# Bidirectional Mamba block: first pairs reordered, polynomial bank changed

## The chip, the cores and the metric

The kernel runs on one core of a Trainium2 chip. The metric is the device time of one execution in microseconds. A core has five engines that run their own instruction queues: TensorE (PE; its weight loads are shown as PEld), VectorE (DVE), ScalarE (ACT), GpSimd (POOL) and SyncE (SP), which here issues most transfers. They wait for each other by semaphores only. TensorE writes to PSUM, 8 banks of 2 KB per partition; GpSimd does not read PSUM in this kernel.

## What is computed

A batch of 8 sequences, 512 tokens, 256 channels, in float32. For each sequence:

```python
x = x + attn(layernorm(x))          # two Mamba2 directions, joined by Wo, bo
x = x + ffn(layernorm(x))           # x @ W.T + b + (x @ V_r) @ C.T

# one direction (the other runs over the flipped sequence)
zxbcdt = x @ Win                                   # 256 -> 512 z, 640 xBC, 8 dt
xBC = silu(conv4_causal_depthwise(xBC) + convb)    # xs 512, B 64, C 64
dt  = softplus(dt + dtb);  dA = exp(dt * -exp(Alog))     # 8 heads
h_t = dA_t * h_(t-1) + dt_t * B_t (x) x_t          # state 64 x 64 per head
y_t = C_t . h_t + D * x_t
y = y * silu(z);  y = y * rsqrt(mean(y*y) + 1e-5) * normw
return y @ Wout
```

## The kernel before, in words

A sequence is cut into 4 chunks of 128 tokens. A **pair** (class `Pair`, L461) is chunk c of the forward direction with chunk 3 - c of the backward one; there are 32 pairs, 4 per sequence. Within a chunk the recurrence is done as matrix products: `lam` (L478) is the decay dA broadcast over 128 partitions for 8 heads, `scan` (L505) turns it into a 128x128 decay matrix per head on VectorE, `cb` (L533) forms the products of C and B on TensorE, `mix` (L544) multiplies both on VectorE, and `outputs` (L582) applies them to `xdt` (x times dt, `scale_x`, L522, GpSimd). Between chunks a state `h` is carried: `add_state`, `new_state`, `decay_state` (L574 to L618), and `dec` (L484, scaled by C in `scale_c`, L498) carries it into the outputs. `evict` (L620, VectorE) adds the skip term, which `skip` (L549, ScalarE) has put into `yg`; `times_gate` (L624, GpSimd) multiplies by the gate, which `gate` (L557, TensorE) and `gate_silu` (L569, ScalarE) have made.

A **Block** (L388) is 128 channels of the xBC projection of one direction over the whole sequence: block 4 holds B and C, blocks 0 to 3 hold x. `project` is TensorE (L401), `tap` (L411, ScalarE) does the first conv tap out of PSUM, `convolve` (L414) the other three on VectorE, or `convolve_aside` (L424) does them as three ScalarE products and three GpSimd additions. `silu` (L434) follows on ScalarE, for a whole block of 512 tokens. While the pairs of one sequence run, the ten blocks of the next are made, spread by the table `share` (L826 to L833).

Step sizes are made for two sequences at a time (class `Steps`, L308): softplus by a polynomial of 9 terms on VectorE (`ratio`, L318, and `series`, L326), whose intermediates z and u lie in one PSUM bank, `pzu` (L319); then `exponential` on ScalarE and `decays` (L340), which writes the decays to DRAM; from there the broadcasts `lam` and `dec` are fetched by SP (`fetch`, `fetch_dec`).

A **Tail** (L650) is one finished chunk of 128 tokens: the output product with `wy` (L664), which is Wout, normw and Wo multiplied beforehand in `prepare_wy` (L196), then residual, second norm and the feed-forward product.

PSUM: one bank holds the identity `seed` for the scans; `p_proj` has 3 banks, `p_tr` (transposes, cb, small things) 2, `p_y` 2. A pool gives out the bank whose release was recorded first, so the order of the program decides which release a matmul waits for.

Nothing is planned at run time. The order on each engine is the order in which the program is written, fixed by `pin` (L60): first the start (L721 to L820), which norms sequence 0 (L724 to L733), transposes it (L738), makes its blocks and the step sizes of sequences 0 and 1, and prepares pair 0; then the loop over the pairs (L849), which finishes pair i and prepares pair i + 1. SP's queue is in order too: the loads of weights (`load_weights`, L178) put two of them, `wot`, into buffers of the pool of `lam`, so later `lam` fetches wait until those are free.

Of the kernel before, what the change touches and what calls it, by code (L numbers as in the profile page):

```python
# [14 lines left out]
P = 128  # L15
# [16 lines left out]
def tile_bimamba_ffn(  # L32
# [163 lines left out]
    def prepare_wy(d, blks):  # L196

        wot, wo_sb = staged[d]
        for blk in blks:
            pw = ps(p_y, [P, DM], f"pwy_{d}_{blk}")  # L200
            for k in range(NK):
                pe.matmul(
                    pw, lhsT=wot[:, k, blk * P:(blk + 1) * P], rhs=wo_sb[:, k, :],
                    start=(k == 0), stop=(k == NK - 1),
                )
            dve.tensor_scalar(wy[:, d, blk, :], pw, normw_sb[:, d, blk:blk + 1], None, ALU.mult)
# [18 lines left out]

    def scales(mv, n, name):

        rs = small.tile([P, n], F32, name=f"{name}_rs", tag=f"lnrs{n}")
        nm = small.tile([P, n], F32, name=f"{name}_nm", tag=f"lnnm{n}")
        pool.tensor_scalar(rs, mv[:, :, 1], 1.0, EPS, ALU.mult, ALU.add)  # L230
        pool.tensor_tensor(rs, rs, neghalf[:, :n], ALU.pow)
        pool.tensor_tensor(nm, mv[:, :, 0], rs, ALU.mult)
        pool.tensor_scalar(nm, nm, -1.0, None, ALU.mult)
        return rs, nm
# [73 lines left out]
    class Steps:  # L308
# [9 lines left out]
        def ratio(m):  # L318
            pzu = ps(p_tr, [P, 2, P], f"pzu_{m.b0}")  # L319
            m.z, m.u = pzu[:, 0, :], pzu[:, 1, :]  # L320
            dve.tensor_scalar(m.z, m.e, 2.0, None, ALU.add)
            dve.reciprocal(m.r, m.z)
            dve.tensor_tensor(m.e, m.e, m.r, ALU.mult)
            dve.tensor_tensor(m.u, m.e, m.e, ALU.mult)
# [136 lines left out]
    class Pair:  # L461
# [51 lines left out]

        def turn(m, d):
# [18 lines left out]
        def cb(m):  # L533

            m.pcb = [ps(p_tr, [P, P], f"cb_{m.name}_{d}") for d in range(2)]
            for u in range(2):
                for d in range(2):
# [19 lines left out]
        def gate(m, d):  # L557
            if d == 0:
                m.sz = m.tile("sz", (P, 2, NBLK, P))
# [7 lines left out]
            m.pz = pz  # L567

        def gate_silu(m, d):  # L569
            act.activation(m.sz[:, d], m.pz, AF.Silu)  # L570
# [79 lines left out]
    class Tail:  # L650
# [37 lines left out]
        def norm2_v(t):  # L688

            rs = small.tile([P, 1], F32, name=f"ln2_{t.name}_rs", tag="lnrs1")  # L690
            pool.tensor_scalar(rs, t.mv[:, :, 1], 1.0, EPS, ALU.mult, ALU.add)
            pool.tensor_tensor(rs, rs, neghalf[:, :1], ALU.pow)
# [33 lines left out]
    for c0 in range(0, NC, 2):  # L726
        mv = statistics(xh[:, c0:c0 + 2], 2, f"ln1_0_{c0}")
        halves.append(scales(mv, 2, f"ln1_0_{c0}"))
    for half, (rs, nm) in enumerate(halves):
        c = 2 * half  # L730
        act.activation(xh[:, c, :], xh[:, c, :], AF.Identity, bias=nm[:, 0:1], scale=rs[:, 0:1])
        c += 1
        dve.tensor_scalar(xh[:, c, :], xh[:, c, :], rs[:, 1:2], nm[:, 1:2], ALU.mult, ALU.add)  # L733
# [9 lines left out]
    for j in range(NC):  # L743
        dve.tensor_copy(seed[:, j * P:(j + 1) * P], ident)

    def projected(*key):
        first[key].project(p_y if key[1] in (2, 3) else None)
        first[key].tap()


    act.activation(a_col, a_col, AF.Exp)
    dve.tensor_scalar(a_col, a_col, -1.0, None, ALU.mult)
    projected(0, NBLK)
    stats1(1, 0)
    stats1(1, 2)
    scales1(1)
    projected(0, 0)
    norm1(1)
    projected(0, 1)
    first[0, NBLK].convolve()  # L760
    projected(0, 2)
    pdt = ps(p_y, [P, P], "pdt_0")
    steps_direct(pdt, 0, 0)
    for k in range(NK):
        turn1(1, k)
    first[0, 1].convolve_aside()
    first[0, 0].convolve()
# [3 lines left out]
    first[0, 2].convolve()  # L771
    st.ratio()
    first[0, 3].convolve_aside()
    st.series()
    projected(1, NBLK)
    projected(1, 0)
    st.exponential()
    first[1, NBLK].convolve()
# [10 lines left out]
    first[0, NBLK].silu()  # L789
    first[1, 1].convolve_aside()  # L790
    projected(1, 2)
    first[1, 0].convolve()
    projected(1, 3)
    for blk in range(NBLK):
        first[0, blk].silu()
    q.gate(0)
    steps_by_token(0)
    q.turn(0)
    first[1, NBLK].silu()
    first[1, 2].convolve()  # L800
    q.cb()
    q.scale_x(0)
    q.gate_silu(0)
    first[1, 0].silu()
    first[1, 3].convolve()
    q.gate(1)
    q.scan(0)
    first[1, 1].silu()
    first[1, 2].silu()
    first[1, 3].silu()  # L810
    q.turn(1)
    q.scale_x(1)
    q.gate_silu(1)
    q.skip(0)
    q.mix(0)
    q.scan(1)
    tokenwise_b(0)
# [7 lines left out]
    for b in range(1, NB):  # L825
# [5 lines left out]
        for bb, c, m in share:  # L831
            todo[bb, c] = [Block(b, *blocks[k + j]) for j in range(m)]
            k += m  # L833
    ends = [(b, c) for b in range(NB) for c in (1, 2, 0, 3)]
# [14 lines left out]
    for i in range(n):  # L849
# [19 lines left out]
        p.decay_state()  # L869
        if q:  # L870
            q.scale_c()
# [15 lines left out]
        when(work[0], "project", "tap")  # L887
# [25 lines left out]
        if i < 2:  # L913
            prepare_wy(i, range(2))
# [10 lines left out]
        when(before, "norm_power")  # L925
        p.presum()
# [15 lines left out]
        if i < 2:  # L942
            prepare_wy(i, range(2, NBLK))
        elif i == 2:
            prepare_wf()
        when(work[1], "convolve")
        if i == 0:
            steps_last(0)
            steps_total(0)
# [7 lines left out]
        if q:  # L957
            q.gate(1)
            q.gate_silu(1)
        if even and c in (1, 3) and ahead < NB:  # L960
            turn1(ahead + (c == 3), 0)
            turn1(ahead + (c == 3), 1)
        if q:
            q.skip(1)
        if c == 2 and b + 1 < NB:
            tokenwise_b(b + 1)
        for w in work[2:]:
            when(w, "project", "tap")
        when(work[1], "silu")
        for w in work[2:]:  # L970
            when(w, "convolve")
        if b == 0:
            when(work[3], "silu")
# [3 lines left out]
        late, before = work[2], p  # L977
# [66 lines left out]
```

## Time and profile before

| | |
|---|---|
| time, median of 3 runs | 638.48 us (638.48 to 639.05) |
| the profiled execution | 640.16 us, of which its span 638.4 us |
| TensorE clock granted, mean | 0.99 |
| busy: PE, DVE, POOL, ACT | 96%, 85%, 73%, 61% of the span |
| chain that ended last | PE 72%, DVE 13%, POOL 6%, ACT 4% |
| 0 to 48 us: PE, DVE, ACT, POOL busy | 34.16, 33.48, 29.55, 21.12 us |
| 48 to 110 us: the same | 61.12, 58.65, 40.89, 39.77 us |

The span runs from the first to the last instruction; the time has 1.8 us more around it. The profile names an instruction by line, engine, operation and its tiles, out<-in. A wait is put down to what ended last before the instruction could start. The busy share of an engine is an average over stages, so what counts is which engine the others wait for in each stage; the slices and the busy time by stage show that.

### The profile page before, as it was taken

The page shows a single profiled execution, that of the slowest core. Times are in us where ns is not written, and L with a number is a line of the kernel's source. Part 1 is how long each engine was busy: PE and PEld are TensorE (multiplying, and loading weights), DVE is VectorE, ACT ScalarE, POOL GpSimd, SP SyncE. Part 2 cuts the span into 40 slices and gives each one's busy share as a digit, 9 for nine tenths or more (in the row PEclk, how much of TensorE's full clock was granted, in tenths as well). Part 3 has the DMA queues.
Part 4 walks back from the last instruction along what each step waited for, and adds up shares of the span by engine and source line. Part 5 has one row for each costly group of instructions (what it writes and reads, how often), then busy time and mean ns, then how long its engine had stood idle before and what let it go on. Part 6 is the DMA issues. An engine that isn't in the chain of part 4 may idle for free.

```text
span 638.4 us, 12802 instructions
## 1 busy us (share of the span) xinstructions
PE 612.1 (96%) x4772; PEld 459.5 (72%) x4772; DVE 542.4 (85%) x827; ACT 392.3 (61%) x845; POOL 464.6 (73%) x570
## 2 busy tenths in 40 slices
PE   4979999999999999999999999999999999999896
PEld 2547677678777787767777787767777778788784
DVE  4798999989999988888999989887999998866733
ACT  2787656767676465766776574774786665644431
POOL 3548664778767895867857897766868788589982
PEclk9989999999999999999999999999999999999998
DMA  7464432035055423017056322107026232343011
GB/s 217 143 195 139 132 101 49 2 103 166 1 190 150 116 83 116 17 32 223 18 160 164 102 94 77 59 20 216 18 55 204 66 99 83 117 138 96 16 51 34
DMA packets 36254, 64.87 MB, mean 102 GB/s; under 512 B 8608, under 2 KB 23392, under 8 KB 36192
## 3 DMA queue, kind: packets, MB, share of 16 engines
q1 hardware_dynamic: 34048, 64.00, 33.3%
q8 instruction: 38, 0.62, 0.4%
q10 hardware_dynamic: 2144, 0.04, 0.2%
q14 instruction: 24, 0.20, 0.1%
HBM read 59.12 MB, written 4.72 MB: 100 GB/s over the span
## 4 chain that ended last, share of the span: by engine, by line
PE 72%; DVE 13%; POOL 6%; ACT 4%; issue 3%; DMA 1%; ACTq 0%; POOLq 0%; DVEq 0%
PE pp L401 18%; PE pm L669 14%; PE pz L563 14%; PE py L588 8%; PE pf L709 4%; PE pxs L518 4%; DVE lam L512 3%; DVE xc L419 2%; PE pst L608 2%; PE ss L634 2%; PE cb L539 2%; DVE lam L545 1%; DVE r L330 1%; POOL yg L626 1%; POOL xdt L529 1%
## 5 line engine op out<-in xcount | busy, mean ns | idle before, releaser
L419 DVE SCALAR_TENSOR_TENSOR xc<-pp,conv_sb,xc 128x511 f32<-128x511 f32 x183 | 135.8, 745 | 28.0 <-ACT xc L412 23.6
L401 PE MATMUL pp<-xhT,win_sb 128*128 128x512 f32 x320 | 151.3, 600 | 0.5 <-ACT xhT L739 0.5
L512 DVE TENSOR_TENSOR_SCAN lam<-lam,seed 128x512 f32<-128x512 f32 x128 | 145.6, 1200 | 0.0
L563 PEld LDWEIGHTS pz<-xhT,win_sb 128*128 128x128 f32 x1024 | 123.3, 194 | 10.6 <-issue 9.4
L563 PE MATMUL pz<-xhT,win_sb 128*128 128x128 f32 x1024 | 126.9, 278 | 0.0
L669 PE MATMUL pm<-wy,yg 128*128 128x256 f32 x512 | 115.6, 379 | 0.0
L669 PEld LDWEIGHTS pm<-wy,yg 128*128 128x128 f32 x512 | 97.1, 190 | 13.3 <-issue 0.2
L401 PEld LDWEIGHTS pp<-xhT,win_sb 128*128 128x128 f32 x320 | 57.6, 193 | 45.9 <-issue 43.3
L553 ACT ACTIVATE yg<-xc,dcol 128x128 f32<-128x128 f32 x256 | 81.3, 395 | 0.0
L412 ACT ACTIVATE xc<-pp,conv_sb 128x512 f32<-128x512 f32 x64 | 49.5, 777 | 47.4 <-PE pp L401 47.4
L545 DVE TENSOR_TENSOR lam<-lam,cb 128x1024 f32<-128x1024 f32 x64 | 75.0, 1212 | 0.3
L529 POOL TENSOR_TENSOR xdt<-xs,dw 128x512 f32<-128x512 f32 x64 | 66.5, 1045 | 6.5 <-ACT xs L520 6.4
L588 PE MATMUL py<-lam,xdt 128*64 128x128 f32 x1024 | 63.0, 276 | 0.0
L588 PEld LDWEIGHTS py<-lam,xdt 128*64 128x64 f32 x1024 | 55.2, 137 | 9.2 <-issue 3.1
L622 DVE TENSOR_TENSOR yg<-py,yg 128x512 f32<-128x512 f32 x64 | 42.0, 684 | 14.9 <-PE py L588 13.2
L529 POOL TENSOR_TENSOR xs<-xs,dw 128x512 f32<-128x512 f32 x48 | 50.1, 1043 | 3.8
L676 DVE SCALAR_TENSOR_TENSOR x<-pm,rms,x 128x256 f32<-128x256 f32 x64 | 30.8, 482 | 18.5 <-PE pm L669 8.2
L638 ACT ACTIVATE rms<-ss,eps_col 128x2 f32<-128x2 f32 x32 | 8.4, 262 | 61.9 <-PE ss L634 61.8
L437 ACT ACTIVATE xc<-xc 128x512 f32<-128x512 f32 x64 | 39.4, 626 | 11.0 <-DVE xc L419 10.9
L518 PE MATMUL pxs<-ident,xc 128*128 128x128 f32 x256 | 39.1, 285 | 6.8 <-ACT xc L437 4.2
L230 POOL TENSOR_SCALAR ln_rs<-ln_mv 128x1 f32<-128x1 f32 (+2 forms) x39 | 7.5, 192 | 48.9 <-DVE ln_mv L223 47.9
L520 ACT COPY xs<-pxs 128x512 f32<-128x512 f32 x64 | 35.9, 589 | 11.4 <-PE pxs L518 11.4
(446 smaller groups left out, 999.3 us busy)
## 6 DMA issues: line engine op xcount, KB each, us to landing
lam<-dat SPq DMA_DIRECT2D x64, 512.0 KB
x<-in_x_dram SPq DMA_DIRECT2D x36, 128.0 KB
out_dram<-x SPq DMA_DIRECT2D x32, 128.0 KB
x<-in_x_dram SPq DMA_DIRECT2D x7, 512.0 KB
win_sb<-in_win_dram SPq DMA_DIRECT2D x2, 640.0 KB
win_sb<-in_win_dram SPq DMA_DIRECT2D x2, 512.0 KB
wot<-in_wout_t_dram SPq DMA_DIRECT2D x2, 512.0 KB
rows<-raw SPq DMA_DIRECT2D x48, 4.0 KB
```

Source lines behind the costliest of these rows:

```text
L401: pe.matmul(pp, lhsT=win_sb[:, d, k, c0:c0 + P], rhs=s["xhT"][:, k, :], start=(k == 0), stop=(k == NK - 1),)
L412: act.activation(self.acc, self.pp, AF.Identity, bias=self.w[:, 4:5], scale=self.w[:, 3:4])
L419: dve.scalar_tensor_tensor(self.acc[:, to], self.pp[:, of], self.w[:, 3 - j:4 - j], self.acc[:, to], ALU.mult, ALU.add,)
L512: dve.tensor_tensor_scan(lam, lam, sd, 0.0, ALU.mult, ALU.add)
L518: pe.transpose(pt[:, blk * P:(blk + 1) * P], m.s["xc", d][:, blk, m.tcol[d]], ident)
L529: pool.tensor_tensor(hb(to), hb(m.xw[d]), dw[:, j, cols].unsqueeze(2).to_broadcast([P, NH, HD]), ALU.mult)
L545: dve.tensor_tensor(m.lam[d], m.lam[d], m.pcb[d].unsqueeze(1).to_broadcast([P, NH, P]), ALU.mult)
L553: act.activation(yg[:, blk, :], m.s["xc", d][:, blk, m.tcol[d]], AF.Copy, scale=dcol[:, d, blk:blk + 1])
L563: pe.matmul(pz[:, blk, :], lhsT=win_sb[:, d, k, blk * P:(blk + 1) * P], rhs=m.s["xhT"][:, k, m.tcol[d]], start=(k == 0), stop=(k == NK - 1),)
L588: pe.matmul(m.py[d][two * HD:(two + 1) * HD, blk, :], lhsT=lhsT, rhs=rhs, start=first, stop=last, skip_group_check=True,)
L622: dve.tensor_tensor(yg, m.py[d], yg, ALU.add)
L669: pe.matmul(t.pm[:, d, :], lhsT=yg[:, blk, :], rhs=wy[:, d, blk, :], start=(blk == 0), stop=(blk == NBLK - 1),)
```

## The change

- **First norm.** Sequence 0 is normed wholly on VectorE, as (x - mean) times the inverse deviation, instead of two chunks on ScalarE and two on VectorE as x times scale plus offset. The offsets are not made any more. The four copies of the identity into `seed` go from VectorE to ScalarE.
- **Start reordered.** The statistics of sequence 1 stand ahead of the multiplication of `a_col`; `tap` and `convolve` are called apart from `project`; block 1 of the forward direction is convolved on VectorE, block 3 of the backward one aside; the convs of the backward direction come after `decays`.
- **Silu of x by chunk.** For sequence 0 the silu of x is done chunk by chunk (`silu_x`, all four blocks of 128 tokens at once), for pairs 0 and 1 in the start, for pairs 2 and 3 at the end of the loops two pairs earlier.
- **Output weights ahead.** `prepare_wy` makes two blocks in one bank. Direction 0 is made in the start, its scaling on ScalarE; direction 1 in the first loop; `prepare_wf` moves from the third loop to the second. The first block of sequence 1 is projected and tapped in the start (`ahead`).
- **Within sequence 0's loops.** `scale_c` comes after the scans, `decay_state` at the end of the loop before, one block of sequence 1 is convolved aside in the first loop, and its B and C blocks get their silu one loop later ("late").
- **Polynomial.** For the sequences after the first two, `pzu` is taken from `p_proj` instead of `p_tr`.
- `cb` issues direction 0's two products before direction 1's; `m.pz` keeps both gates' banks.

```diff
-    def prepare_wy(d, blks):
+    def prepare_wy(d, blks, aside=False):
         wot, wo_sb = staged[d]
-        for blk in blks:
-            pw = ps(p_y, [P, DM], f"pwy_{d}_{blk}")
+        pw = ps(p_y, [P, 2, DM], f"pwy_{d}_{blks[0]}")
+        for j, blk in enumerate(blks):
...
+            if aside:
+                act.activation(to, pw[:, j, :], AF.Copy, scale=scale)
+            else:
+                dve.tensor_scalar(to, pw[:, j, :], scale, None, ALU.mult)
...
         def ratio(m):
-            pzu = ps(p_tr, [P, 2, P], f"pzu_{m.b0}")
+            pzu = ps(p_proj if m.b0 else p_tr, [P, 2, P], f"pzu_{m.b0}")
...
+        def silu_x(m, d):
+            x = m.s["xc", d][:, :, m.tcol[d]]
+            act.activation(x, x, AF.Silu)
...
-    for half, (rs, nm) in enumerate(halves):
-        c = 2 * half
-        act.activation(xh[:, c, :], xh[:, c, :], AF.Identity, bias=nm[:, 0:1], scale=rs[:, 0:1])
-        c += 1
-        dve.tensor_scalar(xh[:, c, :], xh[:, c, :], rs[:, 1:2], nm[:, 1:2], ALU.mult, ALU.add)
+    for half, (mv, rs) in enumerate(halves):
+        for j in range(2):
+            c = 2 * half + j
+            dve.tensor_scalar(xh[:, c, :], xh[:, c, :], mv[:, j, 0:1], rs[:, j:j + 1], ALU.subtract, ALU.mult)
...
-    for j in range(NC):
-        dve.tensor_copy(seed[:, j * P:(j + 1) * P], ident)
+    for j in range(NC):
+        act.copy(seed[:, j * P:(j + 1) * P], ident)
     act.activation(a_col, a_col, AF.Exp)
-    dve.tensor_scalar(a_col, a_col, -1.0, None, ALU.mult)
-    projected(0, NBLK)
     stats1(1, 0)
     stats1(1, 2)
     scales1(1)
+    projected(0, NBLK)
+    tap(0, NBLK)
...
     projected(0, 3)
-    first[0, 2].convolve()
+    tap(0, 3)
     st.ratio()
     first[0, 3].convolve_aside()
+    projected(1, NBLK)
+    tap(1, NBLK)
     st.series()
-    projected(1, NBLK)
     projected(1, 0)
+    tap(1, 0)
     st.exponential()
-    first[1, NBLK].convolve()
     st.decays()
     st.weigh()
...
-    for blk in range(NBLK):
-        first[0, blk].silu()
+    q.silu_x(0)
+    first[0, NBLK].silu()
+    first[1, 3].convolve_aside()
     q.gate(0)
+    q.gate(1)
     steps_by_token(0)
     q.turn(0)
+    conv(1, 2)
+    q.scale_x(0)
     first[1, NBLK].silu()
-    first[1, 2].convolve()
+    prepare_wy(0, (0, 1), True)
+    tokenwise_b(0)
     q.cb()
-    q.scale_x(0)
     q.gate_silu(0)
-    first[1, 0].silu()
-    first[1, 3].convolve()
-    q.gate(1)
+    q.silu_x(1)
     q.scan(0)
-    first[1, 1].silu()
-    first[1, 2].silu()
-    first[1, 3].silu()
+    pairs[1].silu_x(0)
+    prepare_wy(0, (2, 3), True)
     q.turn(1)
+    ahead = Block(1, *blocks[0])
+    ahead.project()
     q.scale_x(1)
     q.gate_silu(1)
+    pairs[1].silu_x(1)
+    ahead.tap()
+    steps_last(0)
     q.skip(0)
...
+        if i + 2 < NC:
+            for d in range(2):
+                pairs[i + 2].silu_x(d)
...
-        when(work[1], "silu")
-        for w in work[2:]:
-            when(w, "convolve")
-        if b == 0:
-            when(work[3], "silu")
+        if i:
+            when(work[1], "silu")
+        if q and q.b == 0:
+            q.decay_state()
+        when(work[2], "convolve")
+        when(work[3], "convolve_aside")
...
-        late, before = work[2], p
+        late, before = work[2:] if i else work[1:], p
```

## The prediction

> **What bounds the kernel now.** I read the busy shares and slices first, then the chain that ended last, busy time by stage, the waits of the engine that the chain names, and last the first 60 us in order of time.
>
> ```profile
> PE 612.1 (96%) x4772; PEld 459.5 (72%) x4772; DVE 542.4 (85%) x827; ACT 392.3 (61%) x845; POOL 464.6 (73%) x570
> PE   4979999999999999999999999999999999999896
> PE 72%; DVE 13%; POOL 6%; ACT 4%; issue 3%; DMA 1%; ACTq 0%; POOLq 0%; DVEq 0%
> ```
>
> TensorE carries 72% of the chain and is full from the fourth slice (48 us) to about 560 us. The change touches nothing after that, so a microsecond counts if it is TensorE idle time ahead of 48 us, or a gap later.
>
> ```profile
> 60.00:75.00 15.00, 14.80 (x121) 10.02 (x120) 14.62 (x28) 8.87 (x19) 9.26 (x11) 1.00 0.27 88
> 75.00:90.00 15.00, 15.00 (x115) 10.82 (x115) 14.21 (x22) 11.55 (x25) 11.70 (x11) 1.00 0.32 99
> 90.00:110.00 20.00, 20.00 (x182) 13.95 (x177) 19.65 (x30) 11.51 (x26) 9.23 (x12) 1.00 0.35 87
> 200.00:300.00 100.00, 100.00 (x790) 74.25 (x787) 88.45 (x127) 62.70 (x139) 76.91 (x92) 1.00 0.35 103
> ```
>
> Columns: the stage and its length, then PE, PEld, DVE, ACT and POOL busy, clock, DMA share, GB/s. From 60 to 110 us (the pairs of sequence 0) TensorE and VectorE are full together; later TensorE alone is.
>
> ```profile
> PE pxs L518 <- DVE dt L333: 1.4, 3, 0.5
> PE pxs L518 <- ACT rms L638: 1.1, 3, 0.4
> ```
>
> These are six of TensorE's seven own waits between 75 and 560 us (total us, times, longest), all while the step-size polynomial holds a bank of `p_tr`. The start, in order of time (start, length, and in brackets the idle time before):
>
> ```profile
> 8.43 1.97 PE L738 MATMUL pxh<-ident,x 128*128 128x128 f32 x8 [8.43 <-ACT x L731]
> 10.86 9.23 PE L401 MATMUL pp<-xhT,win_sb 128*128 128x512 f32 x16 [0.46 <-ACT xhT L739]
> 14.01 0.20 ACT L751 ACTIVATE a_col<-a_col 128x1 f32<-128x1 f32 x1 [3.20 <-DMA a_col<-in_heads_dram]
> 31.35 1.29 DVE L332 TENSOR_SCALAR dt<-v 128x128 f32<-128x128 f32 x1
> 40.62 0.33 PE L518 MATMUL pxs<-ident,xc 128*128 128x128 f32 x1 [2.77 <-ACT xc L437]
> 45.11 3.78 PE L563 MATMUL pz<-xhT,win_sb 128*128 128x128 f32 x16
> ```
>
> TensorE waits for the first norm until 8.43, and stands almost idle from 37.9 to 44.5 waiting for silu; after that hole the gates at 45.11 take 3.78 us where the same 16 matmuls at 35.61 took 2.02.
>
> **The change, part by part.** Line numbers are those of before; times are us of the profiled execution.
>
> *First norm.* Removed: two GpSimd operations per half (0.19 + 0.23), two ScalarE norms (1.09) behind a 1.28 table load. Added: two VectorE norms (0.41 each). Statistics end at 5.98; the second half's factor follows by 0.19 + 0.72 at 7.05, two norms end at 7.9, two chunk transposes and the copy give xhT at 9.2 instead of 10.82: 1.6 earlier. ScalarE then still stands until the a_col transfer at 14.0, so its first tap moves from 14.68 to 14.2 only; the seed copies moved to it (4 x 0.29) lie inside that wait. TensorE ran its first matmuls at 1.22 against 0.59 us until about 15.5. If it speeds up at that same time, the earlier start is worth half, 0.8; if as long after its start as before, 1.6.
>
> *Step sizes.* Sequence 1's statistics no longer stand behind a_col on VectorE (they began at 14.32), so its norm ends at 17.8 to 18.6, not 20.65, and the second half of the dt product starts when TensorE gets there, 21.4 to 22.5 (was 22.98). The exponential ends 24.3 to 25.4 (was 26.39); VectorE, now doing block 1's taps too (2.3), is free at the same time. The polynomial chain was 26.42 to 33.28, 6.86. It holds one fast L332 stretched from 0.21 to 1.29, ending just after GpSimd's add at 32.55; the add moves along. r is ready at T = 31.5 to 32.6; I take 32.0, a gain of 1.3. Decays come straight after, not behind a conv (2.3) and a tap (0.8): ended at T + 1.4 = 33.4, not 36.4. The broadcasts of lam follow 3 us earlier; the weights' transfers end at 33.3, so the queue is free, and lam needs about 4 us from its issue (38.11 to 42), so at 39.2, with VectorE's three convs (3 x 2.22) ending at 40.1. Cover 0.9; if it went, the scan would be late by as much, but it waits for the product cb after that anyway.
>
> *ScalarE from T to the first eviction.* exp 0.33, tap 0.67, 3 tmp 1.84, 2 taps 1.35, table 1.28, silu of one chunk 0.55, two B/C halves 1.28, 3 tmp 1.84, dw and xs 0.95, two halves 1.28, 2 output weights 0.85 (bounded by L248's 0.52 and L377's 0.38), bn 0.4, gate 0.55, two chunk silus 1.06, wait for the next two weights' products 0.5, those 0.8, xs 0.55, gate 0.55, chunk 0.55, tap 0.67, last 0.7, two skips 2.34: 20.9. So the second skip ends at 52.9 (skip was 53.39), and the second eviction at 53.6 against 54.16: 0.6 gained, though TensorE's own outputs end some 2 us sooner. GpSimd's third set of adds (3 x 1.32), ahead of the first scale_x, ends at 44.2 and costs no more.
>
> *Moved out of the full stage.* VectorE loses, between 54 and 110, one block's convs (2.22, now 1.84 on ScalarE and 3.95 on GpSimd) and four output-weight scalings (1.7). TensorE loses four output-weight products (3.7), now run between 40 and 46.5 where it was idle. VectorE is the tighter: 3.9. Against it stands GpSimd: its pair-0 loop is now gates 2.5, scale_x 4.2, dec 2.4, presum 2.0, step-ahead norm 1.7, state 1.0 and adds 4.0, 17.8, about VectorE's 17.1; and pair 1's gates, scale_x and dec stand behind the adds, so dec for pair 2 ends at about 83.7 (it was 71.4), just when TensorE wants it. Nearest rows for such a wait: 0 (dec was early) and 2.74 (GpSimd's own wait before pair 1's gates). I take 1.0. Sum at 110 us: 0.6 + 3.9 - 1.0 = 3.5. From there TensorE is full, so it stays to the end.
>
> *Polynomial's bank.* The transposes no longer wait for L333 (1.4) nor, one transpose earlier, fully for rms (1.1). Instead the gates of the next pair wait for that bank: they start at 166.89, the bank is free at 164.42, a slack of 1.7 after the gain. Bounds 0 and 2.5; the slack covers it, so 2.0.
>
> *Nothing for the rest.* Gate 1 ahead of the transposes fills idle TensorE. dec for pair 1 is scaled after scale_x: ready near 61, wanted near 66; without that cover TensorE would wait 2.4. Late silu of B/C: used a sequence later. Output weights' products need transfers landed by 33. On SP's queue, lam of pair 2 and one of pair 3 now wait for the weights' buffers (last used near 46 and 60); they are scanned at 72 and 90, so 8 us of cover, and SP's later issues move no later.
>
> Sum: 3.5 + 2.0 = 5.5. The profiled execution took 640.16 (span 638.4, 1.8 around it), so 634.7 for such a one; the median shown is 638.48, 1.7 lower, so **633.0**.
>
> **A rule against a row.** The Trainium skill (SBUF — State Buffer, Who interferes with whom) says that a VectorE tensor_scalar in a two-port mode and a GpSimd operation block each other whole. L332 agrees. By that rule the new norms would stand behind GpSimd's power (0.72), and the sum would be 4.8. L733, the same form with two column operands, took 0.41 with GpSimd's operations beside it at full pace, so I leave it out.
>
> **Rivals.**
>
> *The hole stays cold.* TensorE's granted clock was 0.50 from 42.7 to 49.1, in spite of four transposes in the hole. Now it has holes of about 1 us around the weight products. For: they leave it half idle from 41 to 45. Against: the weight products fill 3.7 of it. Price: 2.0 to 2.7 (3.78 - 1.78 per such group), mostly on the path: 635.5. The Trainium skill (TensorE: Matmul & The Clock Gate, Part 1) has the clock halve after one idle window of some 3.4 us; the row agrees, though that window was not quite idle.
>
> *Everything overlaps well.* The start gains the full 1.6, GpSimd's wait is nil, the polynomial gives 2.5: 630.5. Against: four engines within 1 us of each other at 83 us.
>
> *Hidden.* VectorE's first eviction waits for ScalarE and the relief is eaten in GpSimd's queue; the bank's wait moves to the gates: 638.5.
>
> *Slower: GpSimd takes over in pairs 0 to 2.* Its adds wait for ScalarE's tmp, which stands behind chunk silus, and hold up gates, scale_x and dec. In the walk dec for pair 2 ends 5 us before TensorE started those outputs in the old run (88.66). Beyond 5 us of delay it decides; if ScalarE's waits for each other's gates double the adds and scale_x (8.2), pair 2 is 3 late, less the polynomial's 2: 640. For: GpSimd has 17.8 in a loop of 18. Against: it had 40 of 62 us busy there.
>
> **How the numbers follow.** Forecast 0.45, cold hole 0.17, overlap 0.18, hidden 0.06, slower 0.14. A run of this kernel tells about 0.2% (1.3 us) from no change: faster 0.80, same 0.06, slower 0.14. The range reaches from the overlap case (with 1 us for unknown ends) 629.5 to the edge of the hidden one, 638.0; the likeliest's own is 631.5 to 634.5.
>
> **What would show it.** The first transpose near 6.5 and r near 32; the second eviction near 53.6; VectorE's last conv in pair 2's loop ending near 105, not 108.7; the two waits for L333 and rms gone; granted clock without 0.50 in the forties. Wrong, if GpSimd shows waits of TensorE or VectorE for it between 55 and 90, if lam is waited for, or if the gates wait for the polynomial.

## The result, and the profile after

The kernel after took 632.26 us (median of 5 runs, 631.81 to 635.5) beside 638.8 for the kernel before: a ratio of 0.9902, 95% interval 0.9874 to 0.993, or 6.5 us less. The forecast was 633.0. In a second set of six runs (after_again below) it took 634.08 beside 638.23: 0.9929 [0.9914, 0.9945], 4.2 us less. The gain is real and its size depends on the set: 4 to 6.5 us, with the forecast's 5.5 inside. The profiled execution of after took 632.27 (span 630.2).

The page of after, first its busy times, then TensorE's slices, then the chain that ended last:

```profile
PE 609.0 (97%) x4772; PEld 456.8 (72%) x4772; DVE 538.8 (86%) x818; ACT 395.6 (63%) x854; POOL 467.6 (74%) x569
PE   5989999999999999999999999999999999999896
PE 76%; DVE 10%; POOL 7%; ACT 4%; issue 2%; DMA 0%; SPq 0%; DVEq 0%; POOLq 0%; ACTq 0%
```

TensorE has the same 4772 matmuls. It is full from the fourth slice on, as before, and the third (32 to 47 us) has gone from 7 to 8 tenths. Its share of the chain has gone from 72% to 76% and VectorE's from 13% to 10%. By stage (length, then PE, PEld, DVE, ACT and POOL busy, clock, DMA share, GB/s):

```profile
60.00:75.00 15.00, 14.63 (x127) 10.10 (x125) 14.72 (x27) 10.45 (x22) 11.19 (x13) 1.00 0.46 149
75.00:90.00 15.00, 13.89 (x127) 9.27 (x126) 13.54 (x22) 14.08 (x31) 11.84 (x11) 1.00 0.21 69
90.00:110.00 20.00, 19.90 (x168) 14.51 (x167) 19.72 (x26) 14.10 (x30) 14.82 (x16) 1.00 0.15 37
```

TensorE now idles 1.6 us between 60 and 110 us where it idled 0.2: the pairs of sequence 0 have less work for it, and it waits a little for VectorE. Its three longest waits of its own between 69 and 565 us (total us, times, longest); two more are 0.3 each:

```profile
PE pxs L533 <- ACT xc L447: 0.8, 1, 0.8
PE pz L578 <- DVE xc L429: 0.6, 1, 0.6
PE pxs L533 <- ACT rms L653: 0.5, 1, 0.5
```

No wait for the polynomial is left, and of the waits for rms one, ahead of 110 us. The start, in order of time:

```profile
6.28 2.18 PE L750 MATMUL pxh<-ident,x 128*128 128x128 f32 x8 [6.28 <-DVE x L745]
9.34 7.56 PE L411 MATMUL pp<-xhT,win_sb 128*128 128x512 f32 x12 [0.88 <-ACT seed L766]
31.01 0.84 DVE L344 TENSOR_SCALAR r<-dt,a_col 128x128 f32<-128x128 f32 x1
34.70 3.79 PE L578 MATMUL pz<-xhT,win_sb 128*128 128x128 f32 x32
44.23 0.43 PE L554 MATMUL cb<-cc,bb 64*64 64x128 f32 x4 [0.96 <-ACT bn L466]
52.77 0.69 DVE L637 TENSOR_TENSOR yg<-py,yg 128x512 f32<-128x512 f32 x1 [0.48 <-ACT yg L568]
```

The transposes start 2.15 us earlier, both groups of gates run at full clock (3.79 for 32 matmuls), r is ready at 31.85 and the second eviction ends at 53.46.

Where did the time come from? One matmul row per pair (the first product with a decayed state) gives marks that are the same in both kernels. Their start in us, in four executions that run the old start (bank_only and the two warm runs are described below) and three that run the new one (pair (1,2) is sequence 1's pair of chunk 2):

| outputs of | before | bank_only | warm_hole | warm_both | after | after_again | fetch_ahead |
|---|---|---|---|---|---|---|---|
| (0,1) | 69.3 | 67.4 | 68.0 | 67.8 | 66.0 | 65.8 | 65.4 |
| (0,3) | 104.9 | 102.9 | 103.5 | 103.0 | 99.4 | 99.2 | 98.8 |
| (1,2) | 158.6 | 156.6 | 157.2 | 156.8 | 153.6 | 153.5 | 152.9 |
| (2,1) | 216.0 | 212.9 | 214.7 | 214.2 | 211.0 | 212.3 | 209.2 |
| (3,3) | 327.8 | 323.5 | 326.5 | 326.0 | 321.6 | 322.9 | 319.9 |
| (6,1) | 512.8 | 507.4 | 511.4 | 510.9 | 505.5 | 506.8 | 503.7 |

Read against the profiled execution of before, after gains 5.5 us by (0,3), loses 0.5 up to (2,1), then gains 1.2 and 1.1 at the two later polynomials, 7.3 in all. But that execution of before is 1.4 to 2.0 us later at (0,3) than three others of the same start. At (6,1) the three executions with the old bank average 511.7, the two of after 506.2: 5.5. Each mark is from one profiled execution, so differences below some 2 us between two columns need care: the start alone moves them by as much.

### The profile page after: what moved, and what is told of

Its sections match the earlier page's. It is cut to its first block, busy times and chain, and to the rows that moved or that the text cites. A ratio compares the mean times of both kernels' runs of the same rounds, so it can differ in the third digit from the quotient of the medians.

```text
span 630.2 us, 12795 instructions
## 1 busy us (share of the span) xinstructions
PE 609.0 (97%) x4772; PEld 456.8 (72%) x4772; DVE 538.8 (86%) x818; ACT 395.6 (63%) x854; POOL 467.6 (74%) x569
## 4 chain that ended last, share of the span: by engine, by line
PE 76%; DVE 10%; POOL 7%; ACT 4%; issue 2%; DMA 0%; SPq 0%; DVEq 0%; POOLq 0%; ACTq 0%
PE pp L411 18%; PE pm L684 15%; PE pz L578 13%; PE py L603 10%; PE pf L722 5%; PE pxs L533 4%; DVE lam L522 3%; PE pst L623 3%; DVE xc L429 2%; PE ss L649 2%; PE cb L554 2%; POOL yg L641 1%; DVE lam L560 1%; PE pxt L715 1%; POOL xdt L544 1%
## 5 line engine op out<-in xcount | busy, mean ns | idle before, releaser
L429 DVE SCALAR_TENSOR_TENSOR xc<-pp,conv_sb,xc 128x511 f32<-128x511 f32 x180 | 133.4, 744 | 24.6 <-ACT xc L422 20.0
L578 PEld LDWEIGHTS pz<-xhT,win_sb 128*128 128x128 f32 x1024 | 121.5, 192 | 11.2 <-issue 7.4
L578 PE MATMUL pz<-xhT,win_sb 128*128 128x128 f32 x1024 | 125.0, 275 | 0.7 <-DVE xc L429 0.6
L411 PEld LDWEIGHTS pp<-xhT,win_sb 128*128 128x128 f32 x320 | 57.5, 193 | 46.7 <-issue 43.1
L691 DVE SCALAR_TENSOR_TENSOR x<-pm,rms,x 128x256 f32<-128x256 f32 x64 | 30.8, 481 | 18.7 <-PE pm L684 8.2
L447 ACT ACTIVATE xc<-xc 128x512 f32<-128x512 f32 x56 | 35.0, 626 | 11.5 <-DVE xc L429 11.4
```

The costliest lines, as they stand in the source:

```text
L411: pe.matmul(pp, lhsT=win_sb[:, d, k, c0:c0 + P], rhs=s["xhT"][:, k, :], start=(k == 0), stop=(k == NK - 1),)
L429: dve.scalar_tensor_tensor(self.acc[:, to], self.pp[:, of], self.w[:, 3 - j:4 - j], self.acc[:, to], ALU.mult, ALU.add,)
L578: pe.matmul(pz[:, blk, :], lhsT=win_sb[:, d, k, blk * P:(blk + 1) * P], rhs=m.s["xhT"][:, k, m.tcol[d]], start=(k == 0), stop=(k == NK - 1),)
```

## The experiments

Four parts of the change were undone or made alone: the bank, the output weights, one convolution and the first norm. The silu by chunk, the new order of the start, `scale_c` and `decay_state` were not, so their shares are not known.

**The bank alone, and everything but the bank.** bank_only is the kernel before with

```diff
-            pzu = ps(p_tr, [P, 2, P], f"pzu_{m.b0}")
+            pzu = ps(p_proj if m.b0 else p_tr, [P, 2, P], f"pzu_{m.b0}")
```

> The kernel before with one edit: the polynomials of the later step sizes (three of the four) keep their two working arrays in a bank of p_proj. Theory, the bank counts in full: the six waits of TensorE's transposes for L333 (1.4 us) and for rms (1.1) go, nothing stands in their place because the bank is free before the next gates, and TensorE is full afterwards, so the time falls by 2.0 to 2.5 us, from 638.8 to about 636.5. Rival, the wait only moves to the gates, which now need that bank: TensorE's waits of the same size stand at the gates and the time stays within 0.5 us of 638.8. The profile is that of the kernel before up to about 111 us, so it also tells whether the granted clock of 0.50 near 43 to 49 us is there in another execution: if so, the gates there take about 3.8 us again, if not, about 2.

bank_back is the kernel after with the opposite edit.

> The kernel after with one edit undone: all four polynomials use a bank of p_tr. Theory, the bank counts in full and adds to the rest: 2.0 to 2.5 us lost, 634.3 to 634.8, with TensorE's waits for the polynomial and for rms back at 1.4 and 1.1 us. Rival, the new order of the later loops hides it: 632.3, with those waits under 0.5 us.

bank_only took 634.77 beside 638.95: 0.9936 [0.9919, 0.9954], 4.2 us less. The marks put its gain in three steps: 1.1 between (1,2) and (2,1), 1.2 before (3,3), 1.1 before (5,3), so 3.4. One step in the kernel before:

```profile
163.35 0.66 PE L518 MATMUL pxs<-ident,xc 128*128 128x128 f32 x4 [0.35 <-ACT rms L638]
164.46 0.66 PE L518 MATMUL pxs<-ident,xc 128*128 128x128 f32 x4 [0.46 <-DVE dt L333]
164.95 1.88 PE L401 MATMUL pp<-xhT,win_sb 128*128 128x512 f32 x4
```

and in bank_only:

```profile
160.85 1.15 PE L518 MATMUL pxs<-ident,xc 128*128 128x128 f32 x8
161.83 1.88 PE L401 MATMUL pp<-xhT,win_sb 128*128 128x512 f32 x4
```

From the sums of squares just ahead (at 162.39 and 160.38) to the projection it is 2.56 against 1.45 us: 1.11 less, where the brackets show only 0.81 of waiting. Eight transposes in one run take 1.15, twice four with a wait between take more than the bracket says. The gates got no wait in exchange. So the bank counts in full and for more than its waits (2.0 to 2.5 us were expected); the rival is out. The granted clock of 0.50 was there in this execution too, from 39.8 to 46.4 us, and its second group of gates took 3.26 us.

bank_back took 637.06 beside 638.95, 0.9965 [0.995, 0.9981]: with the old bank the rest of the change is worth 1.9 us by the medians. By the ratios 4.0 us are lost against after's first set and 2.3 against its second, where 2.0 to 2.5 were expected. Its profile fell on the slowest of its twelve runs (639.24, the others 634.56 to 638.49). In it the first polynomial costs TensorE a far longer wait:

```profile
158.66 0.66 PE L533 MATMUL pxs<-ident,xc 128*128 128x128 f32 x4 [0.35 <-ACT rms L653]
161.06 1.12 PE L533 MATMUL pxs<-ident,xc 128*128 128x128 f32 x4 [1.74 <-DVE dt L343]
161.97 3.62 PE L411 MATMUL pp<-xhT,win_sb 128*128 128x512 f32 x4
```

1.74 in place of 0.46, and the projection behind it takes 3.62 where it takes 1.88 above: the granted clock fell (0.93 over 150 to 200 us). That step cost 4.6 us in this execution, the two later ones 1.1 each as before. The median is 2.2 us lower, so the typical first step probably costs less; that was not profiled.

**Single parts undone.** weights_back puts the output weights back into the loops:

```diff
-    prepare_wy(0, (0, 1), True)
...
-    prepare_wy(0, (2, 3), True)
...
-        if i == 0:
-            prepare_wy(1, (0, 1))
+        if i < 2:
+            prepare_wy(i, (0, 1))
```

(likewise for blocks 2 and 3, and the feed-forward weights one loop later).

> The kernel after with the output weights' products and scalings back in the loops of pairs 0 and 1, scaled on VectorE (eight products in two loops instead of four in one ahead and four in the loop of pair 0). Theory, work is moved from a full stage into idle time: TensorE gets 3.7 us and VectorE 1.7 us more in the loops, TensorE idled only about 1.6 us there, so 2.1 to 3.7 us lost, 634.4 to 636.0. If the hole of TensorE near 40 to 45 us also turns cold, with a granted clock of 0.50 in the forties, another 2 us, 636.4 to 638. Rival, the hole would have been lost anyway and the gain came from the order before 40 us: the products cost what they gain and the time stays within 0.6 us of 632.3.

conv_back returns one convolution to VectorE:

```diff
-        when(work[3], "convolve_aside")
+        when(work[3], "convolve")
```

> The kernel after with the convolution that went to ScalarE and GpSimd in the loop of pair 0 back on VectorE. Theory, VectorE is the tighter engine from 55 to 105 us: it gets 2.22 us more against some 2 us of idle time that it has there, and TensorE ends the loop of pair 2 0.8 to 2.2 us later, 633.1 to 634.5. Rival, GpSimd's queue is the tighter one: it is relieved of 4.0 us and the time is 632.3 or less.

norm_back restores the first norm:

```diff
-        halves.append((mv, inverse(mv, 2, f"ln1_0_{c0}")))
+        halves.append(scales(mv, 2, f"ln1_0_{c0}"))
...
+        act.activation(xh[:, c, :], xh[:, c, :], AF.Identity, bias=nm[:, 0:1], scale=rs[:, 0:1])
+        c += 1
+        dve.tensor_scalar(xh[:, c, :], xh[:, c, :], rs[:, 1:2], nm[:, 1:2], ALU.mult, ALU.add)
```

> The kernel after with the first norm as before (one chunk of each half on ScalarE, one on VectorE, with the negated mean from GpSimd). The first transposes start near 8.4 us and not 6.3. Theory, the first norm is worth only a part of that, since a_col's transfer and TensorE's slow start come later anyway: 0.5 to 0.9 us at the second eviction, time 632.8 to 633.2. Rival, the start is a single chain and all of it is lost: 1.6 to 2.1 us, 633.9 to 634.4. Second rival, nothing is lost (632.3) because the step sizes wait for sequence 1.

after_again is the kernel after, unchanged, in norm_back's set.

> The kernel after itself, for another profile and more runs beside the next three. If its first execution is typical, TensorE's second look at it starts each pair's outputs within 0.3 us of the first (66.0, 83.7, 99.4 us) and the time is 632 to 633. If the start differs between executions as it does in the kernel before (where two executions of the same instructions were 2.0 us apart at 88 us, by a longer slow phase of the first projections and another place of the 0.50 clock), the starts of outputs move by 1 us or more.

The last column of the table gives the marks of the one profiled execution of each.

| run | us (median) | ratio to before | second eviction ends | its marks minus after's at (0,1), (0,2), (0,3), (1,2), (6,1) |
|---|---|---|---|---|
| after | 632.26 | 0.9902 [0.9874, 0.993] | 53.46 | 0 |
| after_again | 634.08 | 0.9929 [0.9914, 0.9945] | 53.23 | -0.2, -0.2, -0.2, -0.1, 1.3 |
| weights_back | 634.83 | 0.9931 [0.9913, 0.995] | 53.36 | -0.1, 1.4, 2.0, 1.5, 2.5 |
| conv_back | 635.66 | 0.9961 [0.9941, 0.998] | 52.49 | -1.0, 2.7, 2.0, 1.5, 1.7 |
| norm_back | 634.53 | 0.9933 [0.9913, 0.9953] | 55.45 | 2.0, 2.0, 2.0, 1.9, 3.3 |

By the times alone little is decided: the intervals of weights_back, norm_back and conv_back all overlap that of after_again. The marks carry the readings that follow, one execution for each run.

weights_back ends its start as after does and loses 2.0 us in the loops of pairs 0 to 2: relief of a full stage, as the theory had it, at its lower end. The granted clock did fall (to 0.50 from about 44.5 to 48 us), but its second eviction is not later for it.

conv_back began 1.0 us early by chance and loses 3.0 by (0,3). Its row for the stage from 75 us:

```profile
75.00:90.00 15.00, 12.01 (x104) 8.56 (x102) 13.83 (x21) 12.87 (x27) 10.03 (x9) 0.89 0.03 5
```

and the wait of TensorE that makes it:

```profile
PE pz L578 <- DVE xc L429: 3.0, 1, 3.0
```

A projection bank stands full until VectorE has done its convolution, TensorE's second gates wait 3.0 us for it, and the clock falls behind that wait (0.52 from 80 to 82 us, 0.89 over the stage). GpSimd is relieved there by 4.0 us of adds and nothing gets faster. So VectorE is the tighter engine, as the theory had it, but the loss of 3.0 is above the 0.8 to 2.2 expected, and the gates behind the wait take 3.51 us at the fallen clock where they take 1.95 at full clock. The twelve times spread from 633.9 to 639.0, and the profile is the fastest of them, so the typical loss may be larger.

norm_back is 2.0 us later than after from the first pair on, nearly all of its later start, as the first rival had it. Its first projections:

```profile
9.04 1.97 PE L751 MATMUL pxh<-ident,x 128*128 128x128 f32 x8 [9.04 <-ACT x L744]
11.47 7.44 PE L411 MATMUL pp<-xhT,win_sb 128*128 128x512 f32 x12 [0.46 <-ACT xhT L752]
```

Twelve projections take 7.44 us from 11.47 and 7.56 from 9.34, as if the slow phase followed TensorE's own start. One pair of executions does not show that, because the length of this phase varies: twelve projections took 6.40 (forms) to 7.64 us (weights_back) in the nine executions with the new norm. In these nine the work behind the twelve starts at 15.8 to 16.8 us, 16.4 on average; in the five with the old norm at 16.8 to 18.7, 17.7 on average. That is 1.3 us apart, and the first projections themselves 1.8. By the medians norm_back (634.53) is only 0.5 us slower than after_again (634.08) of the same set. So the first norm's worth is open, between nothing and 2 us.

after_again itself starts its outputs within 0.2 us of after up to (1,2), as the first case of its expectation had it, but takes 634.08 and not 632 to 633: between (1,2) and (2,1) its execution loses 1.4 us against the first profile of after.

**What eats the gain after 140 us.** From the outputs of (1,2) to those of (1,3) TensorE took 20.8 us in before, 19.7 in bank_only, 20.1 in after and 21.5 in after_again; from there to (2,1) 36.6, 36.6, 37.3 and 37.3. After thus gives back what the bank gives at the first polynomial. GpSimd's longest wait between 120 and 160 us, in after:

```profile
POOL dec__1415 L511 <- DMA dec__1415<-dec: 4.9, 1, 4.9
```

the same in after_again:

```profile
POOL dec__1415 L511 <- DMA dec__1415<-dec: 6.5, 1, 6.5
```

and what SyncE's queue issued in after ahead of that transfer (start, length):

```profile
121.82 11.38 SPq L303 DMA_DIRECT2D rows<-raw  x16
133.31 0.84 SPq L492 DMA_DIRECT2D lam<-dat  x2
134.25 1.13 SPq L499 DMA_DIRECT2D dec__1415<-dec  x2
```

The queue stands until the raw step sizes are made, and then their 16 row transfers hold it for 11.4 us. Behind them stand lam and dec for pair (1,2), although their buffers are free from about 101 us, when fetch_ahead issues them. There they go first (two conditions that keep them from being issued twice are not shown):

```diff
...
+        if even and c == 3:
+            pairs[i + 3] = Pair(*order[i + 3])
+            pairs[i + 3].fetch()
+            pairs[i + 3].fetch_dec()
...
         if even and c == 3 and ahead < NB:
             raw = steps_raw(ahead)
```

> The kernel after, with the transfers of lam and dec for the third pair of each odd sequence given to SyncE's queue ahead of the 16 row transfers of the raw step sizes, and no longer behind them. Theory, part of the gain is given back there: the 16 issues hold SyncE's queue from 121.8 to 133.3 us, dec for pair (1,2) lands only at 141.9 to 143.3, GpSimd waits 4.9 to 6.5 us for it, and with GpSimd late the VectorE and TensorE waits at 150 to 176 us follow. With the transfers ahead, GpSimd's wait is gone, TensorE gets from the outputs of (1,2) to those of (1,3) in about 20 us in place of 20.1 to 21.5 and from (1,3) to (2,1) in 36.6 in place of 37.3; 0.7 to 2 us gained, against 632.3 to 634.1 for the kernel after, thus 631.5 to 632.5. Rival, the same executions lose that time to VectorE, whose polynomial stands there: GpSimd's wait goes, the intervals stay and the time is that of the kernel after.

It took 630.63 (630.57 to 633.42) beside 638.72: 0.9888 [0.9872, 0.9905], a little below the 631.5 to 632.5 expected. Its queue:

```profile
100.98 1.20 SPq L492 DMA_DIRECT2D lam<-dat  x2
102.27 1.09 SPq L499 DMA_DIRECT2D dec__1228<-dec  x2
...
121.20 11.39 SPq L303 DMA_DIRECT2D rows<-raw  x16
```

Its stage from 150 us, and then that of after:

```profile
150.00:200.00 50.00, 50.00 (x413) 38.15 (x412) 48.52 (x82) 36.40 (x76) 35.98 (x43) 1.00 0.37 114
```

```profile
150.00:200.00 50.00, 49.54 (x400) 37.46 (x399) 48.25 (x81) 35.43 (x75) 37.08 (x46) 1.00 0.36 113
```

The transfers are issued at 101 to 103 us, and GpSimd's wait for dec is gone. Its longest wait there is now this one:

```profile
POOL yg L641 <- DMA x<-in_x_dram: 2.5, 1, 2.5
```

The two intervals are 19.8 and 36.5 and TensorE is full. The theory holds and VectorE as the rival cause is out: 1.1 us against the first profile of after and 2.5 against the second, from that stretch alone (fetch_ahead also began 0.6 earlier by chance). The other executions with the new bank for the polynomial say the same:

| run | GpSimd's wait for dec, us | from (1,2) to (2,1), us |
|---|---|---|
| fetch_ahead, better2 (below) | none | 56.3, 56.3 |
| bank_only | 3.2 | 56.3 |
| after, forms (below) | 4.9, 4.9 | 57.4, 57.5 |
| conv_back | 5.1 | 57.6 |
| weights_back, norm_back, better1 (below) | 5.9 each | 58.4, 58.4, 58.3 |
| after_again | 6.5 | 58.8 |

Up to some 3.8 us of the wait is covered by other work (an estimate from these rows), and each us beyond costs TensorE about one. At the two later polynomials GpSimd waits 2.8 to 3.6 us in after, and nothing is lost: the same stretch is 56.3 and 56.4. fetch_ahead's median is the lowest of the study, 0.3 below better2's, which is no difference; against after by the times alone its interval still overlaps that of the first set.

**A wait that was explained wrongly.** The trace has VectorE rows of the polynomial that stretch while GpSimd works (in after 0.84 where L344 takes 0.28 elsewhere). forms writes two of them otherwise:

```diff
-            dve.tensor_scalar(m.dt, m.v, 0.0, None, ALU.max)
+            dve.tensor_tensor(m.dt, m.v, zeros, ALU.max)
...
-            dve.tensor_scalar(m.r, m.dt, a_col[:, 0:1], -1e30, ALU.mult, ALU.max)
+            dve.scalar_tensor_tensor(m.r, m.dt, a_col[:, 0:1], floor, ALU.mult, ALU.max)
```

> The kernel after, with two of the polynomial's 15 VectorE operations in another form: the maximum with zero as a tensor_tensor against a tile of zeros, the product with a_col as a scalar_tensor_tensor against a tile of -1e30. Theory, the tensor_scalar form between two SBUF tiles stands still while GpSimd works: the operation ahead of it is shown at 1.01 to 1.57 us where it takes 0.3, ending 0.16 us after GpSimd's operation, and the product at 0.84 where it takes 0.29. In the new forms r of the first step sizes is ready near 30.7 and not 31.85, and as the start is one chain 0.5 to 1.2 us reach the first outputs; the three later polynomials get 0.5 to 1.2 each where they stand before the evictions. In all 1 to 3 us: 630 to 632.5 beside 632.3 to 634.1. Rival, the stretch is GpSimd's use of the memory and hits any form: the two rows stay stretched, and the time is that of the kernel after.

It took 633.74, 0.9922 [0.9909, 0.9936], like the kernel after. The rows of forms, VectorE first, then GpSimd beside it, then the same pair at the first later polynomial:

```profile
29.80 1.35 DVE L343 SCALAR_TENSOR_TENSOR pzu<-r,e 128x128 f32<-128x128 f32 x1
...
26.89 4.10 POOL L444 TENSOR_TENSOR xc<-xc,tmp 128x511 f32<-128x511 f32 x3 [9.53 <-ACT tmp L443]
...
160.37 1.57 DVE L343 SCALAR_TENSOR_TENSOR pzu<-r,e 128x128 f32<-128x128 f32 x1
...
159.41 2.37 POOL L513 TENSOR_TENSOR dec__1614<-dec__1614,cc 128x1024 f32<-128x1024 f32 x1
```

The stretched row stayed stretched, ending 0.16 us after GpSimd's operation both times, with no tensor_scalar behind it. The theory fell: it is not that form alone. Both forms stretch: in before it was the tensor_scalar L332 (1.29, ending 0.09 after GpSimd's adds), here L343. L343 reads two tiles in SBUF; the seven steps of the series, which read one of their two from PSUM, keep their 0.32 beside the same adds. The Trainium skill (SBUF — State Buffer, Who interferes with whom) has a VectorE instruction with two SBUF inputs contend with a GpSimd instruction that reads SBUF; these rows agree, and the new forms only moved the polynomial from one contending form to another.

**The cold hole.** warm_hole and warm_both are the kernel before with transposes of the identity in TensorE's holes. They write to a bank that the next products overwrite:

```diff
+            if m.name == "0_0" and d == 0:
+                for _ in range(20):
+                    pe.transpose(pt[:, :P], ident, ident)
```

> The kernel before with one addition: 20 transposes of the identity on TensorE in its hole near 38 to 41 us (their result is overwritten by the transposes that follow). They take some 2.6 us and nothing waits for them. Theory, the cold hole costs: the granted clock stays at 1.00 through the forties, the second group of gates takes 2.0 us and not 3.3 to 3.8, the first outputs start 1.3 to 1.8 us earlier, and the time falls to 637.1 to 637.7 from about 638.9. Rival, VectorE bounds that stretch and the gates hide in it: the clock is warm but the first outputs start within 0.4 us of where they did and the time stays at 638.5 to 639.3. Second rival, the drop does not come from idling: 0.50 shows in the forties all the same.

> The kernel before with transposes of the identity in both of TensorE's holes: the 20 of the run warm_hole near 38 to 41 us, and 12 more in the middle of pair 0's first cb group, where it idled 1.35 us near 43. With the first hole alone filled the granted clock still fell, later and for 3.3 in place of 6.5 us. Theory, any idle stretch of 2 us or so is followed by the drop 2 to 5 us later: with both filled the clock is 1.00 through the forties, the gates take 2.0 us in place of 3.3 to 3.8, the first outputs start 1.2 to 1.8 us earlier than in the kernel before, and the time is 637.0 to 637.6 beside 638.5. Rival, the drop is set by something else than idling, such as the time since the start: 0.50 shows in the forties again.

warm_hole took 638.57 beside 638.23: 1.0001 [0.9988, 1.0014]; the clock still fell, from about 44.3 to 47.7 us. warm_both took 638.78 beside 638.72: 0.9995 [0.9983, 1.0007], with the clock at 1.00:

```profile
44.02 2.05 PE L569 MATMUL pz<-xhT,win_sb 128*128 128x128 f32 x16
46.67 0.63 PE L521 MATMUL pxs<-ident,xc 128*128 128x128 f32 x4 [0.59 <-DVE lam L551]
48.45 1.09 PE L594 MATMUL py<-lam,xdt 128*64 128x128 f32 x16
50.19 1.09 PE L594 MATMUL py<-lam,xdt 128*64 128x128 f32 x16 [0.65 <-POOL xs L532]
```

The gates are back at 2.05 us, TensorE then waits for VectorE's mix and GpSimd's xs, and the median is the same. With both holes filled no drop is left in the forties of this execution, which speaks for idling as its cause.

In the old start the drop costs next to nothing, because the slow gates hide behind other engines. From the first product for the step sizes to the outputs of (0,1) it is 48.9 us in bank_only with 6.5 us of drop, in warm_hole with half of it and in warm_both with none; in before, where the drop comes later (42.3 to 49.1 us), it is 49.4. One thing stays open: of warm_both's eleven runs, five have a mean clock of 0.999 or 1.00 and took 637.4 to 638.6, six have 0.996 or 0.997 and took 638.8 to 639.9. Where those six lost it was not profiled.

In the new start that is otherwise, because TensorE is full there. forms is after's program but for those two operations and has nearly the same gaps, but in its profile the clock fell. Two stages of forms, then the second of them in after:

```profile
44.00:46.00 2.00, 1.57 (x9) 1.24 (x10) 2.00 (x3) 1.91 (x5) 1.92 (x2) 0.92 0.84 213
46.00:48.00 2.00, 2.00 (x8) 1.54 (x7) 1.90 (x2) 0.21 (x1) 0.11 (x1) 0.50 0.04 10
```

```profile
46.00:48.00 2.00, 2.00 (x10) 1.34 (x9) 1.90 (x2) 1.37 (x4) 0.00 (x0) 1.00 0.16 57
```

Its second eviction ends at 55.33 and every mark after that is 1.8 to 2.0 us later than after's. So after's spread may be partly this: of its first five runs the one at 635.5 had a mean granted clock of 0.993, the other four 0.998 to 1.00; of the six in the second set, five had 0.993. That those five dropped in the same place was not profiled, and the drop does not make up the second set's slowness: its one execution at 1.00 took 633.71, hardly less than the 633.97 to 635.27 of the others.

**A better order.** better1 lets VectorE's two scans run before the mixes, and ScalarE's skips before a tap that is needed later:

```diff
     q.gate_silu(1)
+    q.skip(0)
     pairs[1].silu_x(1)
+    q.skip(1)
     ahead.tap()
     steps_last(0)
-    q.skip(0)
-    q.mix(0)
     q.scan(1)
+    q.mix(0)
     q.mix(1)
-    q.skip(1)
```

> The kernel after with another order just ahead of the pairs' loop: both scans of pair 0 before its first mix, and its two skips on ScalarE ahead of the next block's tap and the last decays. VectorE waited 3.5 us for the first skip there. Theory: the second eviction ends near 52.0 us and not 53.5, VectorE is 1.4 us earlier into the loop, and TensorE's 1.6 us of waits between 60 and 110 us for VectorE's products shrink by 0.5 to 1.4: 630.9 to 631.8. Rival, TensorE is full from 45 us on and its small waits have other causes (the power of the norm, transfers): 632.0 to 632.5, no change.

better2 has this, fetch_ahead's transfers and the forms of forms.

> The kernel after with the three edits together: the order of better1, the transfers of fetch_ahead, the forms of forms. If the three losses are separate, the gains add: 1.0 to 1.8 (order) and 0.7 to 2 (transfers) and 1 to 3 (forms), 628.5 to 631. If they hide one another, TensorE being full between them, 630.5 to 632.

better1 took 632.18 beside 638.23, 0.9904 [0.9882, 0.9927]: the second eviction ended at 51.65, the marks were 1.0 us early up to (1,2) (0.4 of it there already at the first gates) and the same as after's from (1,3) on: dec for (1,2) gave it all back (GpSimd's wait 5.9). better2 took 630.89, 0.9878 [0.9862, 0.9894], no different from fetch_ahead alone. It lies in both ranges of its expectation, and its execution began 0.6 us later than fetch_ahead's (first product for the step sizes at 16.68 against 16.11) but was only 0.1 to 0.3 later at the marks. So the order may still bring some 0.5 us on top of the transfers; whether the gains add is not shown.

## Why the prediction came out right, step by step

- **First norm.** Transposes near 6.5: 6.28. First tap 14.2: 13.13, since a_col's transfer landed at 12.0 in this execution. Of the two prices left open, 0.8 or 1.6, neither is shown: the means of the fourteen executions lie between them (1.3), norm_back's one execution above (2.0), its median below (0.5). That phase varies by more than a us from one execution to the next, which the text did not allow for. On VectorE the row was right to decide against the rule: the first two norms took 0.73 together from 5.81, while GpSimd's power (0.70 from 6.14) ran beside them.
- **Step sizes.** r at 32.0: 31.85. Decays 33.4: 33.19. The three convs end 40.1: 39.98. GpSimd's third adds 44.2: 43.79. All within 0.5 us. The gain of 1.3 was measured against a late execution, though: in the three others of the old start r was ready at 31.9 to 32.5.
- **ScalarE to the first evictions.** Second skip 52.9: 52.68. Second eviction 53.6: 53.46. Again the times were right and the gain of 0.6 was not: the other old starts end that eviction at 52.1 to 52.8. So against those three the start gained nothing. Part of that is the tap and the last decays, which now stand before the loop: better1, with the skips ahead of them, ends that eviction 1.8 earlier, 0.4 of it from its start. What the weight products cost there was not measured apart.
- **Relief of the full stage.** 3.9 for VectorE, less 1.0 for GpSimd. dec for pair 2 83.7: 83.44, 0.3 ahead of TensorE's use at 83.72. VectorE's last conv 105: 104.90. The wait allowance was not needed: neither TensorE's matmuls nor VectorE wait for GpSimd there. The stage's sum of 3.5 measured 5.5 between the two profiled executions and 4.2 against the mean of the four old starts at (0,3) (103.6). The mis-sized term is the relief: from the second eviction to (0,3) the gain is 4.7 against before and 4.8 against that mean, where the text had 3.9 less 1.0. weights_back and conv_back lose 2.0 and 3.0 there, more than the 1.7 and 2.2 of VectorE's time that they were costed at.
- **Polynomial's bank.** Taken at 2.0 of bounds 0 and 2.5; it measured 3.4 in bank_only's marks and 4.2 by its median. The term was read from the brackets of the waits, and a split run of transposes costs 0.3 more than its brackets each time. In after the first of the three was eaten by a step that I had costed at nothing: SyncE's queue. I gave lam of pairs 2 and 3 their cover, wrote that the queue's later issues move no later, and did not ask what an earlier arrival of the engines does to a transfer whose issue stands behind 16 others.
- **Rivals.** The cold hole did not happen in the profiled run; a drop in the new start costs 1.9 (forms), near the 2.0 of the text. That is partly luck: the price was read from the old start, where it is worth nothing. GpSimd taking over: no matmul and no VectorE operation waits for it between 55 and 90 us. Hidden: bank_only excludes that the bank's wait moves to the gates, and the marks at (0,3) that the relief is eaten. Everything overlaps well: GpSimd's wait was nil and the polynomial gave more than 2.5 in bank_only, as that rival had it, but the start's gain did not show against the other old starts, and SyncE's queue took some back.

Thus the path was right (TensorE full behind a relieved stage, the bank in full), and that the sum came out is partly luck. Two terms were too small (the relief by 1.8 to 1.9, the bank by 1.4), the start's 0.6 did not show against the other old starts, and a loss of 1.1 to 2.5 in SyncE's queue was missing. These errors partly cancel: 5.5 at (6,1) by the marks, 6.5 and 4.2 by the two sets.

## What to carry to other kernels

Before a gain is costed against one profile, look at a second execution of the same instructions: here the start alone varied by 2 us, a third of the effect, while the predicted times of events held to 0.5 us but for the first tap. Where TensorE is full, take a wait's price from the distance between the work before and behind it, not from the bracket. And when a kernel's front gets earlier, go through the in-order DMA queue for transfers that wait behind a longer batch without needing to: that edit, fetch_ahead, was worth 1.1 to 2.5 us by the marks.

## What the runs showed of the hardware that was not expected

- The start of TensorE varies between executions of the same instructions: 16 projections from 10.9 us took 9.23 (before), 7.81 (bank_only) and 8.47 us (warm_hole). In before the first five ran at 0.93 to 1.22 us each, in bank_only the first two at 1.22 and 0.79, and the rest at 0.59.
- The granted clock fell to 0.50 in forms although TensorE's longest idle time between 38 and 46 us was 0.96 us, and not in after with the same gaps. The Trainium skill (TensorE: Matmul & The Clock Gate, Part 1) speaks of one idle window of some 3.4 us; here no gap above 0.96 us was needed in one execution, and the measurement decides.
- A drop of the clock is worth what stands behind TensorE at that place: next to nothing in the old start (48.9 us to (0,1) in bank_only with the drop and in warm_both without it), 1.9 us in the new one (forms).
